# Groups of four in a two-layer conditional MLP: diagonal blocks summed in PSUM, off-diagonal banks begun by VectorE, and sums of shared matrices kept in DRAM

## The chip, the cores and the metric

The kernel runs on one core of one Trainium2 chip. The metric is the device time in microseconds, the median over runs. A profile of one execution comes beside it: it records every instruction of the engines TensorE (PE, with its weight loads as PEld), VectorE (DVE), ScalarE (ACT), GpSimd (POOL) and of the queues that issue DMAs (SP above all).

## The reference, cut to what matters

There are 16 batches x[b] of 256 x 256 numbers and two layers, each added to x.

```python
# layer 0: one expert of 8 for each batch, width 512
up, gate = x @ Wu[e].T + bu[e], x @ Wg[e].T + bg[e]
x = x + (silu(up) * gate) @ Wd[e].T + bd[e]

# layer 1: the two best of 8 experts for each batch, width 1024, weights w,
# and one shared expert that every batch passes through
mlp = lambda x, g, u, d: (gelu(x @ g) * (x @ u)) @ d
x = x + sum(w[k] * mlp(x, *expert[k]) for k in range(2)) + mlp(x, *shared)
```

All of it is float32.

## The kernel before, in words

**Units.** The work is cut into units that share one weight matrix. A *pair* (class Pair) is two batches with the same expert; a *single* (class Single) is one batch. Pairs use a Strassen-like scheme: seven block products (STEPS) in place of eight, from sums of the weight blocks and sums of the data blocks. Layer 0 has 4 pairs and up to 3 more; layer 1 has 12 routed pairs and up to 4 more, and what is left over are singles. The data decide how many: the program has arms for each case (function arms), and here three more pairs of layer 0, three more of layer 1 and two singles of layer 1 run.

The shared expert of layer 1 needs no routing: 8 batches go through it as 4 *shared pairs* (`shared`, which take turns with the three additional pairs of layer 0), the other 8 as two *groups of four* (class Quad) at the end. So the order of the units is: the first two singles and four pairs of layer 0; shared pairs in turn with the additional layer 0 pairs; 15 routed pairs; a single; two groups of four; the last single.

**A quarter of a pair.** The weights of a unit come in quarters j (2 in layer 0, 4 in layer 1). For each, `load_q` loads 512 KB (tile q), `sums_q` has GpSimd form four sums of its blocks (tile s; the operations are lines 588 to 591 in `sums_a`), `up` issues the seven products, and ScalarE (`copy`, L619) and VectorE (`combine`, L627) take the results out of PSUM into c. `act` applies gelu (L684) and the product with the other half (L690), `act_sums` forms three sums of the result with VectorE (`sums_b`, lines 581 to 583). `down` (L728) issues the seven products of the second matrix d, whose sums ds come from `sums_d`, again lines 588 to 591.

**A group of four** multiplies four blocks by four in 26 products instead of 32 (list BLOCK), twice (g = 0, 1). P_i and Q_i give block (i, i) as P_i + Q_i. For each pair i < j the product W goes into a bank that already holds a P (a *seed*, or P itself), ScalarE copies that bank to a second one (L1020), and the products N_ij and N_ji go on top of one bank each; VectorE then closes each with a subtraction (L930). Before the change, P_i and Q_i lie in banks of their own, VectorE adds them for the diagonal block, GpSimd makes "diagonal minus P" for blocks below it (L1012), and ScalarE writes the seeds (L973). `act` of the group takes a finished 2 x 2 of blocks through gelu (L942) and product (L943), and `act_sums` runs `sums_b` on GpSimd, for the second half of the last group on VectorE. The sums of the data blocks are `sums_r` (L868, L870) and `sums` (L883 to L885). The second half of the first group holds its triples back (`self.second`) until the downs of the first half are over.

**What sets the order.** The program is scheduled by hand. Class Line keeps a clock: `main` issues the next product of TensorE and moves the clock on, `later(after, f)` puts f behind that many units (one unit is one matmul call of 256 columns), and `ahead` issues, at the start of each quarter, the loads and sums for later quarters: q five quarters ahead, sums and x three ahead. Each engine works its instructions off in that order. Nearly all loads are issued on SP; the stores that add to the result are issued on GpSimd (L550). PSUM has eight banks, handed out by `bank` in the order in which they were released.

Of the kernel before, what the change touches and what calls it, by code (L numbers as in the profile page):

```python
# [62 lines left out]
SEED, MEAN = "S", "W"  # L63
BLOCK = (
    "P0", "P1", "Q0", "W01", "P2", "Q1", "P3", "N01", "N10", "Q2", "W23", "Q3",
    "W02", "W12", "N23", "N32", "N02", "N20", "W03", "N12", "N21", "W13",
    "N03", "N30", "N13", "N31",
)
SEEDS = {"Q2": ("02",), "W23": ("12",), "N32": ("03",), "N20": ("13",)}
# [6 lines left out]
def kernel(  # L76
# [22 lines left out]
    factors = [dram.tile([P, QW], F32, name=f"factors{j}") for j in range(CHUNKS)]  # L99

# [95 lines left out]
    psum = {"idle": list(range(NBANKS)), "filled": [False] * NBANKS}  # L196
    open_banks = {}

    def bank(of, seeded=False, half=False):
        ok = [i for i in psum["idle"] if psum["filled"][i] or not seeded]  # L200
        i = ok[0]
        psum["idle"].remove(i)
        assert of not in open_banks
        open_banks[of] = i
        psum["filled"][i] = not half
        return banks[i]
# [356 lines left out]
    class Pair(Unit):  # L563
# [3 lines left out]
        first, step = 18, None  # L567
# [10 lines left out]
        @staticmethod  # L578
        def sums_b(t, more, t2, engine=nc.vector):
            tt = engine.tensor_tensor  # L580
            tt(more[:, 0:2, :], t[:, 0:3:2, :], t[:, 2:4, :], ALU.subtract)  # L581
            tt(t2, t[:, C22, :], more[:, 0, :], ALU.add)  # L582
            tt(more[:, 2, :], t[:, C21, :], t2, ALU.subtract)  # L583
# [9 lines left out]
        def sums_q(self, j):  # L593
            s = take("s", QB, of=(self, j))
            s = s[:, :QW].rearrange("p (m k h) -> p m k h", m=2, k=4)
            self.s[j] = s
            q = self.q[j]
            self.sums_a(lambda n: q[:, :, A_AT[n], :], lambda n: s[:, :, S_AT[n], :])

        def sums_d(self):  # L600
            s = take("ds", 4, KPS[1], P, of=self)
            self.ds = s[:, :, : self.kp]
            d, s = self.d, self.ds
            self.sums_a(lambda n: d[:, A_AT[n]], lambda n: s[:, S_AT[n]])

# [112 lines left out]
        def down(self, k):  # L718
# [55 lines left out]
            elif k == 2:  # L774
                early(C12)
            elif k == 4:
                early(C22)
                early(C21)
                done_with((self, "X"))
                late(C22, "Q", -1)  # L780
# [3 lines left out]
            elif k == 6:  # L784
                late(C12, "Q", -1)
                done_with((self, "Q"))
# [15 lines left out]
        def run(self, line, among):  # L802
# [22 lines left out]
            for k in range(7):  # L825
                line.later(self.first + step * k, lambda k=k: self.down(k))

    class Quad(Unit):
# [32 lines left out]
        def sums_r(self):  # L861
# [3 lines left out]
            for i, k in enumerate(RATIOS):  # L865
# [6 lines left out]
        def sums(self, i, j):  # L872
# [10 lines left out]
            v.scalar_tensor_tensor(both, b["P", i], -1.0, b["P", j], ALU.mult, ALU.subtract)  # L883
            v.scalar_tensor_tensor(one, b["Q", j], -d, both, ALU.mult, ALU.add)
            v.scalar_tensor_tensor(two, b["Q", i], d, both, ALU.mult, ALU.add)  # L885
            b["W", i, j], b["N", i, j], b["N", j, i] = both, one, two

        def first_sums(self):
            if hasattr(self, "xb"):
                self.sums_r()  # L890
                self.sums(0, 1)
# [9 lines left out]
        def sums_d(self):  # L901
            self.ds = take("ds", 4, self.kd, P, of="quads")
            d, s = self.d, self.ds
            Pair.sums_a(lambda n: d[:, A_AT[n]], lambda n: s[:, S_AT[n]])

        def start(self):
            self.bank, self.copies, self.c, self.left, self.second = {}, {}, {}, {}, []
            for h in self.halves:
                h.start()
# [15 lines left out]
        def drop(self, g, *names):  # L925
            for n in names:
                give("cp4", (self, g, n))

        def close(self, g, i, j, dst, a, src, op):
            nc.vector.tensor_tensor(dst, a, src, op)  # L930
            at = g, i // 2, j // 2
            self.left[at] -= 1
            if self.left[at] == 0:
                line.later(3 * UP, lambda: when_free("at", lambda: self.act(*at)))

        def act(self, g, half, pair):
# [11 lines left out]
            if pair == 0 or h.sums_in == "sx":  # L948
                line.later(3 * UP, sums)
# [3 lines left out]
        def act_sums(self, h, j, t):  # L953
            more = take(h.sums_in, 3, S, of=(h, j))
            h.acts[j] = t, more
            engine = nc.vector if h.sums_in == "sx" else nc.gpsimd
            Pair.sums_b(t, more, t[:, 2, :], engine)
# [13 lines left out]
        def seed(self, g, i, j):  # L971
            x = bank((self, g, "X", i, j), seeded=True)
            nc.scalar.activation(x, self.copies[g, f"P{j}"], AF.Copy)  # L973
            self.bank["X", i, j] = x

        def product(self, n):
# [6 lines left out]
            def mm(dst, fresh):  # L983
# [6 lines left out]
            sub, add = ALU.subtract, ALU.add  # L990
            cp = self.copies
            if kind == "P":
                (i,) = ij
                of = (self, g, "X", i, i + 1) if i % 2 == 0 else (self, g, name)
                t = bank(of)
                mm(t, True)
                self.copy(g, name, t)
                if i % 2 == 0:
                    self.bank["X", i, i + 1] = t
                else:  # L1000
                    done_with(of)
            elif kind == "Q":
                (i,) = ij
                t = bank((self, g, name))
                mm(t, True)
                if i != 2:
                    self.copy(g, name, t)
                dst = self.block(g, i, i)
                self.close(g, i, i, dst, cp[g, f"P{i}"], t, add)
                done_with((self, g, name))  # L1010
                for k in ((1,), (), (3, 0, 1), (0, 1))[i]:
                    nc.gpsimd.tensor_tensor(self.block(g, k, i), dst, cp[g, f"P{k}"], sub)  # L1012
                if i == 3:
                    self.drop(g, "P0", "P1")
            elif kind == "W":
                i, j = ij
                x = self.bank["X", i, j]
                mm(x, False)
                y = bank((self, g, "Y", i, j), seeded=True)
                nc.scalar.activation(y, x, AF.Copy)  # L1020
                self.bank["Y", i, j] = y
            else:
                i, j = ij
                lo, hi = min(ij), max(ij)
                inside = hi - lo == 1 and lo % 2 == 0
                which = "X" if inside == (i < j) else "Y"
                t = self.bank.pop((which, lo, hi))
                mm(t, False)
                dst = self.block(g, i, j)
                self.close(g, i, j, dst, cp[g, f"Q{j}"] if which == "X" else dst, t, sub)  # L1030
                done_with((self, g, which, lo, hi))
                for q, last in (("Q1", "N31"), ("Q0", "N30"), ("Q3", "N23")):
                    if name == last:
                        self.drop(g, q)
            for pair in SEEDS.get(name, ()):
                self.seed(g, *map(int, pair))
                if pair == "12":
                    self.drop(g, "P2")
                elif pair == "13":
                    self.drop(g, "P3")  # L1040

        def run(self, line, among):

            self.start()
            while not hasattr(self, "b"):
                line.clock += 1
                line.flush(line.clock)
                self.first_sums()
# [4 lines left out]
            if self is quads[-1]:  # L1053
                give("xb", "quads")
                self.halves[-1].last = True
                if self.alone:
                    line.later(22 + 6 * 5, self.halves[-1].load_z)
            for i, h in enumerate(self.halves):
                for k in range(7):
                    line.later(22 + 6 * (7 * i + k), lambda h=h, k=k: self.down(h, k))  # L1060
# [5 lines left out]
    class Single(Unit):  # L1066
# [75 lines left out]
        def piece(self, line, j, among=False):  # L1142
# [5 lines left out]
            if self.layer:  # L1148
                line.later(SINGLE_UP, lambda: self.down(j))
# [154 lines left out]
    class Line:  # L1304
# [15 lines left out]

        def flush(self, until):
# [8 lines left out]
        def ahead(self, i):  # L1330
# [31 lines left out]
            if u.width == 4:  # L1362
                if j == 0:
                    self.later(0, lambda: u.sums(2, 3))
# [227 lines left out]
```

## Time and profile before

| | us |
|---|---|
| median of 3 runs (1054.15 to 1056.24) | 1054.78 |
| the profiled execution | 1053.92 |
| its span, first to last instruction | 1052.3 |
| end of the last matmul record in the span | 1046.3 |
| TensorE busy | 1030.9 |
| VectorE busy | 788.4 |
| GpSimd busy | 627.5 |
| ScalarE busy | 381.8 |
| bytes moved by DMA, MB (not us) | 143.37 |

The span is shorter than the time by 1.6 us, which lies around the first and the last instruction. Every matmul call leaves two records, so the 4714 records are about 2360 calls; in an undisturbed stretch one record follows the other by 0.216 us, and a call takes 0.43. Durations of matmuls in the tables are longer than that since consecutive ones overlap. A group of lines gives line, engine, operation, what is written and read, and the mean time of one; an arrow in brackets names what ended the idle time ahead of an instruction.

### The profile page before, as it was taken

The numbers are of one execution on the slowest core, as the hardware profiler recorded it, in microseconds if no ns is written. First come the engines' busy times: TensorE is split into PE (matmuls) and PEld (weight loads), VectorE is DVE, ScalarE is ACT, GpSimd is POOL, SyncE is SP. The second block draws the span as 40 slices with busy tenths as digits, with TensorE's granted clock in tenths as the row PEclk, the third lists the DMA queues.
The fourth block names the chain that finished last, engine by engine and source line by source line (L and its number), as shares of the span: only waits on it lengthen the run. The fifth ranks groups of instructions, "written<-read, shape, count | busy, mean of one in ns | idle before, by whom it ended". The sixth has DMA issues, their size and how long they took to land.

```text
span 1052.3 us, 14470 instructions
## 1 busy us (share of the span) xinstructions
PE 1030.9 (98%) x4714; PEld 896.9 (85%) x4714; DVE 788.4 (75%) x1206; ACT 381.8 (36%) x609; POOL 627.5 (60%) x672
## 2 busy tenths in 40 slices
PE   9999999899999999999999999999999999989997
PEld 7888788787878888888888888888888888878786
DVE  8898999879787878878777777778777655685351
ACT  2444353434333333333333333333333314544310
POOL 3955657465474889789567557737763203944821
PEclk9999999999999999999999999999999999999999
DMA  7645515344363665566235534524442364733414
GB/s 267 216 141 184 179 61 160 101 126 154 102 178 140 156 185 146 176 184 175 84 98 140 140 100 101 141 95 115 134 133 88 90 182 133 200 117 100 130 21 75
DMA packets 67508, 143.37 MB, mean 136 GB/s; under 512 B 7890, under 2 KB 38482, under 8 KB 64594
## 3 DMA queue, kind: packets, MB, share of 16 engines
q1 hardware_dynamic: 54866, 129.89, 37.0%
q0 software_dynamic: 12256, 12.06, 9.5%
q8 instruction: 43, 0.70, 0.3%
q14 instruction: 55, 0.45, 0.2%
q10 hardware_dynamic: 288, 0.26, 0.1%
HBM read 114.41 MB, written 27.79 MB: 135 GB/s over the span
## 4 chain that ended last, share of the span: by engine, by line
PE 81%; DVE 8%; POOL 4%; issue 3%; DMA 3%; ACT 1%; SPq 0%; POOLq 0%; DVEq 0%; ACTq 0%
PE bank L642 45%; PE bank L728 27%; PE bank L985 5%; PE bank L1075 3%; DVE c L627 2%; PE bank L1108 1%; DMA d<-wd_dram 1%; DVE bt L690 1%; DVE bt L943 1%; DVE bt L581 1%; DVE bt L582 1%; POOL d L1012 1%; PE bank L224 1%; POOL bt L582 0%; DMA out_dram<-ys 0%
## 5 line engine op out<-in xcount | busy, mean ns | idle before, releaser
L619 ACT ACTIVATE cp<-bank 128x512 f32<-128x512 f32 x270 | 160.9, 596 | 424.3 <-PE bank L642 423.7
L642 PE MATMUL bank<-xt,s 128*128 128x256 f32 x1216 | 288.7, 380 | 7.5 <-DVE c L627 7.5
L642 PEld LDWEIGHTS bank<-xt,s 128*128 128x128 f32 x1216 | 230.1, 190 | 42.3 <-issue 8.0
L627 DVE TENSOR_TENSOR c<-cp,bank 128x512 f32<-128x512 f32 x360 | 233.4, 678 | 31.0 <-ACT cp L619 17.9
L642 PE MATMUL bank<-xt,q 128*128 128x256 f32 x912 | 219.7, 379 | 0.0
L728 PE MATMUL bank<-bt,ds 128*128 128x256 f32 x816 | 196.2, 379 | 2.8 <-POOL bt L582 2.3
L642 PEld LDWEIGHTS bank<-xt,q 128*128 128x128 f32 x912 | 173.3, 190 | 23.6
L690 DVE TENSOR_TENSOR bt<-c 128x1024 f32<-128x1024 f32 x90 | 129.7, 1442 | 78.4 <-ACT c L684 75.9
L728 PEld LDWEIGHTS bank<-bt,ds 128*128 128x128 f32 x816 | 154.7, 190 | 25.1 <-POOL bt L582 2.7
L591 POOL TENSOR_TENSOR s<-s,q 128x256 f32<-128x256 f32 x90 | 77.6, 862 | 121.8 <-PE bank L642 121.8
L588 POOL TENSOR_TENSOR s<-q 128x256 f32<-128x256 f32 x90 | 90.8, 1008 | 86.3 <-PE bank L642 55.8
L728 PE MATMUL bank<-bt,d 128*128 128x256 f32 x572 | 137.0, 379 | 0.0
L728 PEld LDWEIGHTS bank<-bt,d 128*128 128x128 f32 x572 | 108.8, 190 | 15.0 <-DVE c L930 0.2
L550 POOL DMA_DIRECT2D out_dram<-ys x46 | 50.3, 1217 | 91.2 <-DVE ys L757 60.2
L589 POOL TENSOR_TENSOR s<-s,q 128x256 f32<-128x256 f32 x90 | 86.9, 965 | 7.1
L590 POOL TENSOR_TENSOR s<-q 128x256 f32<-128x256 f32 x90 | 86.5, 961 | 0.4 <-PE bank L642 0.4
L684 ACT ACTIVATE c<-c 128x1024 f32<-128x1024 f32 x76 | 79.9, 1052 | 12.5 <-DVE c L627 12.4
L581 DVE TENSOR_TENSOR bt<-bt 128x512 f32<-128x512 f32 x97 | 79.2, 817 | 0.3 <-DMA bt<-x_dram 0.3
L583 DVE TENSOR_TENSOR bt<-bt 128x256 f32<-128x256 f32 x90 | 63.6, 707 | 3.1
L582 DVE TENSOR_TENSOR bt<-bt 128x256 f32<-128x256 f32 x90 | 59.3, 659 | 3.1
L985 PE MATMUL bank<-xt,q 128*128 128x256 f32 x224 | 51.5, 380 | 2.7 <-DVE c L930 2.7
L985 PEld LDWEIGHTS bank<-xt,q 128*128 128x128 f32 x224 | 42.4, 190 | 8.9 <-DVE c L930 3.1
(212 smaller groups left out, 1109.0 us busy)
## 6 DMA issues: line engine op xcount, KB each, us to landing
q<-wq_dram SPq DMA_DIRECT2D x98, 512.0 KB, 3.6
d<-wd_dram SPq DMA_DIRECT2D x19, 1024.0 KB, 6.1
q<-factors SPq DMA_DIRECT2D x26, 512.0 KB, 3.3
xt<-x1d SPq DMA_DIRECT2D x46, 256.0 KB, 5.2
out_dram<-ys POOLq DMA_DIRECT2D x46, 256.0 KB, 6.0
d<-wd_dram SPq DMA_DIRECT2D x7, 513.0 KB, 5.2
bt<-x_dram SPq DMA_DIRECT2D x14, 256.0 KB, 4.6
x1d<-ys SPq DMA_DIRECT2D x14, 256.0 KB, 2.8
```

The source lines that it names most:

```text
L581: tt(more[:, 0:2, :], t[:, 0:3:2, :], t[:, 2:4, :], ALU.subtract)
L588: tt(s("S1"), a("A21"), a("A22"), ALU.add)
L589: tt(s("S2"), s("S1"), a("A11"), ALU.subtract)
L590: tt(s("nS3"), a("A21"), a("A11"), ALU.subtract)
L591: tt(s("nS4"), s("S2"), a("A12"), ALU.subtract)
L619: nc.scalar.activation(t, self.banks["X", j], AF.Copy)
L627: nc.vector.tensor_tensor(self.c[j][:, block].rearrange("p m s -> p (m s)"), self.copies[n, j], self.banks[tag, j], op,)
L642: nc.tensor.matmul(self.banks[tag, j][:, bass.ts(m, S)], lhsT=self.q[j][:, m, A_AT[a], :] if a in A_AT else self.s[j][:, m, S_AT[a], :], r ...
L684: nc.scalar.activation(u, u, AF.Gelu_apprx_tanh)
L690: nc.vector.tensor_tensor(t[:, 0:4, :], u, v, ALU.mult)
L728: nc.tensor.matmul(d, lhsT=src[:, j, :], rhs=self.act_block(j, b), start=OPENS[k] and j == 0, stop=j == self.kp - 1, skip_group_check=True,)
L985: nc.tensor.matmul(dst[:, bass.ts(m, S)], lhsT=w[:, m, :], rhs=rhs, start=fresh and m == 0, stop=True, skip_group_check=True,)
```

## The change

In the shared pairs, only the first computes the sums s and ds; GpSimd stores them to DRAM, and the other three shared pairs load them on SP's queue. The groups of four load ds too.

In the groups of four Q_i accumulates on P_i's bank, so a bank holds the whole diagonal block; ScalarE copies it once for the later subtractions and once more into c (`whole`). Every one of the six W banks is now begun by VectorE as P_i + P_j (`seed`); GpSimd's "diagonal minus P" goes. `act_sums` is VectorE's throughout. The order BLOCK, the seeds' places, the times of the data sums (SUMS_AT, now in single steps), of the activation (ACT_AT, ACT_SUMS_AT) and the order and times of the first group's downs (DOWNS, DOWNS_AT) are new. The downs get banks of their own around the groups (`psum["halves"]`), the last pair's downs come closer together (first 14, step 3), the first group waits until the pairs' downs are issued, and the last single's downs come four units later.

```diff
+BLOCK = ('P0', 'P1', 'P2', 'Q0', 'P3', 'W01', 'Q1', 'Q2', 'W02', 'N01', 'N10', 'Q3', 'W23', 'N02', 'N20', 'W12', 'N32', 'N23', 'W13', 'W03', 'N21', 'N13', 'N12', 'N03', 'N31', 'N30')
+SEEDS = {'P1': ('01',), 'P2': ('02',), 'W02': ('23',), 'Q3': ('12',), 'W12': ('03',), 'N10': ('13',)}
+SUMS_AT = ((4, (0, 2)), (4, (1, 2)), (10, (2, 3)), (22, (1, 3)), (30, (0, 3)))
+DOWNS = (0, 2, 4, 1, 5, 3, 6)
+DOWNS_AT = (8, 11, 12, 15, 19, 25, 27, 27, 33, 39, 46, 48, 49, 50)
+ACT_AT, ACT_SUMS_AT = 10, 6
...
+    qsums = [dram.tile([P, QW], F32, name=f"qsums{j}") for j in range(KPS[1])]
+    dsums = dram.tile([P, 4 * KPS[1] * P], F32, name="dsums")
...
     def bank(of, seeded=False, half=False):
         ok = [i for i in psum["idle"] if psum["filled"][i] or not seeded]
+        if psum["halves"]:
+            ok = [i for i in ok if (i in psum["halves"]) == half]
...
         def sums_q(self, j):
...
+            if self.at is None and self is not shared[0]:
+                nc.sync.dma_start(flat, qsums[j])
+                return
             q = self.q[j]
             self.sums_a(lambda n: q[:, :, A_AT[n], :], lambda n: s[:, :, S_AT[n], :])
+            if self is shared[0]:
+                nc.gpsimd.dma_start(qsums[j], flat)
...
+            if self.apart_banks:
+                line.later(self.first - 2, lambda: psum.update(
+                    halves=sorted(psum["idle"], key=lambda i: psum["filled"][i])[:3]
+                ))
...
-                line.later(3 * UP, lambda: when_free("at", lambda: self.act(*at)))
+                line.later(ACT_AT, lambda: when_free("at", lambda: self.act(*at)))
...
-            engine = nc.vector if h.sums_in == "sx" else nc.gpsimd
-            Pair.sums_b(t, more, t[:, 2, :], engine)
+            Pair.sums_b(t, more, t[:, 2, :])
...
             x = bank((self, g, "X", i, j), seeded=True)
-            nc.scalar.activation(x, self.copies[g, f"P{j}"], AF.Copy)
+            p = [self.copies[g, f"P{k}"] for k in (i, j)]
+            nc.vector.tensor_tensor(x, *p, ALU.add)
...
+        def whole(self, g, i):
+            nc.scalar.activation(self.block(g, i, i), self.copies[g, f"Q{i}"], AF.Copy)
...
             elif kind == "Q":
-                (i,) = ij
-                t = bank((self, g, name))
-                mm(t, True)
-                if i != 2:
-                    self.copy(g, name, t)
-                dst = self.block(g, i, i)
-                self.close(g, i, i, dst, cp[g, f"P{i}"], t, add)
-                done_with((self, g, name))
-                for k in ((1,), (), (3, 0, 1), (0, 1))[i]:
-                    nc.gpsimd.tensor_tensor(self.block(g, k, i), dst, cp[g, f"P{k}"], sub)
+                t = self.bank.pop(ij)
+                mm(t)
+                self.copy(g, name, t)
+                done_with((self, g, *ij))
+                line.later(0, lambda: self.whole(g, *ij))
...
-            while not hasattr(self, "b"):
+            while not hasattr(self, "b") or self is first_quad and line.busy(Pair):
...
-            for i, h in enumerate(self.halves):
-                for k in range(7):
-                    line.later(22 + 6 * (7 * i + k), lambda h=h, k=k: self.down(h, k))
+            for n in range(14):
+                i, k = divmod(n, 7)
+                h = self.halves[i]
+                at = 22 + 6 * n if self is quads[-1] else 2 * DOWNS_AT[n] + 2
+                k = k if self is quads[-1] else DOWNS[k]
+                line.later(at, lambda h=h, k=k: self.down(h, k))
...
-                line.later(SINGLE_UP, lambda: self.down(j))
+                line.later(SINGLE_UP + 4 * bool(self.x_from), lambda: self.down(j))
...
+            last_pair = [*tails[1], *more_pairs[:k]][-1]
+            last_pair.first, last_pair.step, last_pair.apart_banks = 14, 3, True
```

`sums_d` is changed as `sums_q` is, with dsums; in the groups of four it is one load of dsums.

## Prediction, made before the changed kernel was built or run

> **What bounds the kernel now.** I read the page first: busy shares, then the chain.
>
> ```profile
> PE 1030.9 (98%) x4714; PEld 896.9 (85%) x4714; DVE 788.4 (75%) x1206; ACT 381.8 (36%) x609; POOL 627.5 (60%) x672
> ...
> PE 81%; DVE 8%; POOL 4%; issue 3%; DMA 3%; ACT 1%; SPq 0%; POOLq 0%; DVEq 0%; ACTq 0%
> ```
>
> TensorE (PE) is the bound, and the change keeps its work: both orders of BLOCK hold 26 products (8 P and Q, 6 W, 12 N), each two matmuls. So the only thing to win is time in which PE waits or runs slowly. The view of waits, kept to PE, says where that is (total, times, longest):
>
> ```profile
> PE bank L642 <- DVE c L627: 7.5, 6, 2.7
> PE bank L985 <- DVE c L930: 2.7, 1, 2.7
> PE bank L728 <- POOL bt L582: 2.3, 1, 2.3
> ```
>
> Stretches of 20 us place them (stretch, its length, then busy time and count of PE, PEld, DVE, ACT, POOL, the granted clock, DMA share, GB/s). Undisturbed stretches hold 93 to 95 matmul records, these fewer:
>
> ```profile
> 120.00:140.00 20.00, 17.85 (x81) 14.61 (x80) 18.60 (x26) 9.74 (x15) 11.32 (x13) 1.00 0.51 171
> ...
> 180.00:200.00 20.00, 17.32 (x72) 14.40 (x71) 18.54 (x27) 9.94 (x15) 11.67 (x14) 0.91 0.47 158
> ...
> 240.00:260.00 20.00, 18.25 (x82) 15.16 (x82) 18.64 (x23) 10.25 (x15) 13.73 (x15) 1.00 0.37 124
> ...
> 920.00:940.00 20.00, 17.01 (x77) 14.18 (x76) 19.44 (x34) 9.79 (x17) 7.26 (x7) 0.99 0.42 138
> ```
>
> The first three lie where shared pairs alternate with layer 0's pairs, the fourth in the groups of four. In all four VectorE (DVE) is busy over 90%. From 420 to 840, in the routed pairs, PE never waits.
>
> Why is VectorE late there? Its timeline ahead of the wait that ends at 128.51 (start, length), and GpSimd's (POOL) beside it:
>
> ```profile
> 122.63 0.69 DVE L581 TENSOR_TENSOR bt<-bt 128x512 f32<-128x512 f32 x1
> 123.35 0.83 DVE L582 TENSOR_TENSOR dz<-bt 128x256 f32<-128x256 f32 x1
> 124.22 0.84 DVE L583 TENSOR_TENSOR bt<-bt,dz 128x256 f32<-128x256 f32 x1
> 124.98 1.75 DVE L1428 TENSOR_TENSOR z<-z,ys 128x1024 f32<-128x1024 f32 x1
> 126.65 1.21 DVE L690 TENSOR_TENSOR bt<-c 128x1024 f32<-128x1024 f32 x1
> ```
>
> ```profile
> 123.17 0.73 POOL L588 TENSOR_TENSOR s<-q 128x256 f32<-128x256 f32 x1 [0.94 <-PE bank L642]
> 123.98 0.79 POOL L589 TENSOR_TENSOR s<-s,q 128x256 f32<-128x256 f32 x1
> 124.74 0.91 POOL L590 TENSOR_TENSOR s<-q 128x256 f32<-128x256 f32 x1
> ```
>
> L582 and L583 take 0.43 when GpSimd is silent (at 120.63 and 121.09) and twice that here; 1024 elements take 1.21 alone (L690) and 1.75 beside L590. VectorE and GpSimd slow each other when both read SBUF.
>
> **Shared pairs: sums loaded instead of computed.** Counting L588 in order, the sums at 123 are those of the second shared pair, at 174 to 184 of the third, at 240 to 243 of the fourth: all three become loads. Removed from GpSimd: 12 quarters x 4 operations of about 0.95 (L588 to L591) = 45 us, and 3 x 5.4 = 16 us of L588 to L591 on ds. What PE gets back, wait by wait:
> - at 126: 0.40 + 0.41 + 0.54 = 1.35 of a wait of 1.82. VectorE has no gap since 112, where another L583 took 0.83, so I take 1.6;
> - at 184: the L583, L582, L583 from 179.81 each lose 0.41 and the L690 at 175.29 (1.57) 0.36: 1.6 of 2.68. An L581 of 1.52 at 167.12 lay beside the same pair's ds sums; I take 2.1;
> - at 243: 0.47 + 0.53 + 0.54 are more than the wait of 1.50: 1.5;
> - waits of 0.20, 0.33 and 0.24 at 175, 135 and 252, and 0.82 at 301 (behind an L583 of 1.38 beside ds sums that go): 1.3 of 1.59, the rest lying beside GpSimd work that stays.
>
> After the wait at 184 PE itself is slower:
>
> ```profile
> 187.28 1.10 PE L642 MATMUL bank<-xt,s 128*128 128x256 f32 x4 [2.68 <-DVE c L627]
> 188.22 1.58 PE L642 MATMUL bank<-dz,s 128*128 128x256 f32 x4
> 189.60 3.06 PE L642 MATMUL bank<-bt,s 128*128 128x256 f32 x8
> ```
>
> Elsewhere four records take 1.03 and eight 1.89, so this costs 0.55 + 1.17 = 1.7. Of the waits, the two of 2.68 (here and at 935) were followed by this, those of 2.32 and 1.82 were not. With 2.1 gone the wait is 0.6, so I count the 1.7 too. Together 1.6 + 2.1 + 1.5 + 1.3 + 1.7 = **8.2 us**; bounds 4.5 (1.35 + 1.6 + 1.5, clock and the rest unchanged) and 9.3 (all of it).
>
> The Trainium skill (TensorE: Matmul & The Clock Gate, Part 1) has the clock halve only after an idle window of about 3.4 us. By it a wait of 2.68 would not do this and the two slow stretches (3.4 us in all) would stay, leaving 10.8 of the 14.2 worked out here; the rows show slow matmuls behind exactly these two waits, and I go by them.
>
> Added: 12 loads of 512 KB, 4 of 1 MB, and one store of each sum. Today's q loads land 3.6 us after issue, d loads 6.1; these are issued three quarters before use, some 27 us (q loads follow each other about 9 us apart). DMA's share in the three stretches above is 0.37 to 0.51. All go through SP's queue, where the next q load stands behind them; it is five quarters early, and the slot they wait for was freed before the q slot that SP waits for already (539.8 us of SP's waits are that). The five stores cost GpSimd about 1.2 us each (L550). I cost all this at nothing; without that cover one late load is 3.6 us.
>
> **Groups of four.** Their waits: 0.31 at 920, 2.68 at 935, 2.32 at 978, and behind 935 eight records in 3.57 instead of 1.89, 1.7 us; with slow restarts (0.3) 7.3 us. The wait at 935 ends behind a burst of L883 to L885, two of them 1.38 and 1.49 instead of 0.42, beside GpSimd's L1012 and L581; the new SUMS_AT spreads these sums, and both GpSimd operations go. The wait at 978 is for GpSimd's L582, postponed sums of the second half.
>
> What VectorE takes over. The stretch of the products today:
>
> ```profile
> 870.00:1001.00 131.00, 125.69 (x573) 109.18 (x572) 79.73 (x121) 55.37 (x93) 80.39 (x68) 0.99 0.45 132
> ```
>
> Off VectorE: 16 diagonal closes of 0.685 = 11.0, and the slowing of L884, L885 and L943 (2.3 + 1.1 + 2.4 by their means against 0.42 and 1.23) = 5.8. On it: 24 seeds and 12 triples of L581 to L583. A sum of two SBUF tensors into a bank is not in the trace: below it 0.42 (256 elements), above it 0.82 (L581 on bt); I take 0.685 of L930, same shape and one bank: 16.4 (10 to 20). A triple is 1.52 from start to start where GpSimd is silent (1001.89 to 1003.41): 18.2. Net +17.8, so 97.5 busy. Without its waits PE needs 131 - 7.3 = 123.7, so VectorE fills 79%.
>
> ScalarE loses 16 seeds and gains 4 copies of Q and 16 block copies: 4 x 0.6 = 2.4 us on top of 55.4. GpSimd loses 24 L1012 and 12 triples, nearly all it does here.
>
> [...]
>
> What is late next: the four postponed triples, now one VectorE burst of 4 x 1.52 = 6.1 in the second group. The next seed behind it, after an activation product of 1.2, has until W02: six products of 0.86 and three downs of 1.73 = 10.4 us. The burst, product and seed need about 8.5 after the late sum in front. So close, but covered. The downs get two banks of their own, and k=4 stands one product (0.86) behind k=2, whose ScalarE copy takes 0.38 plus what is queued: a few tenths, twice. I charge 1.3 for such new waits: **6.0 us** gained, bounds 7.3 gained and, below, 17.8 lost.
>
> The last pair's downs move from steps of 6 to 3; PE does the same work there without waits today (845 to 900 is full), so nothing. The last single's downs come four units later, but its last still stands between the same two downs, so the chain that ends the kernel (its store, the z load, 0.2 of wait) stays.
>
> **Sum.** The profiled execution took 1053.92 (span 1052.3 and 1.6 around it). 1053.92 - 8.2 - 6.0 = 1039.7; the median of the runs shown is 0.86 higher: **1040.6**.
>
> **Rivals.**
> - *VectorE becomes the bound of the groups.* Today it idles 51.3 of the 131 us, in order behind PE, ScalarE's copies and gelu. If those waits stay while its work grows by 17.8, the stage takes 148.8 and the kernel 1039.7 + 6.0 + 17.8 = 1063.5, or 1064.4. For it: the waits on gelu (8.4) and copies (7.0) are real ones; most new work stands in the same queue as the closes that free banks. Against: over half of its idle time is waiting for PE, which more work simply fills. Slower than before from 42 us of remaining waits (97.5 + 42 = 131 + 8.5).
> - *The groups break even* (33.5 us of waits remain): 1039.7 + 6.0 + 0.9 = 1046.6.
> - *The shared stage gains nothing*, since GpSimd's remaining sums move into the same places or the loads hold SP up: 1039.7 + 8.2 + 0.9 = 1048.8. For it: at 301 and 308 PE waits behind sums that stay. Against: at 184 and 243 no other sums are ready to run.
> - *It does neither*: waits move only: 1054.8.
>
> **Chances.** Forecast 0.57, break-even groups 0.16, no gain in the shared stage 0.13, neither 0.05, VectorE-bound 0.09. A measurement of this kernel can tell about 0.2% (2.1 us) from no change. Faster 0.86, same 0.05, slower 0.09. The range goes from all listed waits gone (9.3 + 7.3: 1038.2) less 1.2 for what the views don't list, 1037.0, to just past the third case, 1049.5; 0.14 is left out.
>
> **What would show it.** Right: PE waits on L627 between 110 and 260 fall below 2 us, L582 and L583 there near 0.43; 93 or more records in each stretch of the groups; VectorE near 80% busy there. Wrong: new waits of PE for a seed or for s loaded from qsums, SP's q loads landing late, VectorE over 95% in the groups.

## The result, and the profile after

The changed kernel takes **1035.46 us** (median of 4 runs, 1034.93 to 1035.97) beside 1054.47 for the kernel before on the same chip (4 runs, 1052.51 to 1056.24). The ratio is 0.982, 95% interval 0.9802 to 0.9839: faster by 1.8%. The prediction was 1040.6 with a range of 1037.0 to 1049.5. Its direction and its places held, its size did not: 19.0 us came where 14.2 were forecast, and the time lies 1.5 us below the range.

The profiled execution took 1034.93 with a span of 1033.3. Its busy shares, and the shares of the chain that ended last:

```profile
PE 1025.3 (99%) x4714; PEld 894.5 (87%) x4714; DVE 786.9 (76%) x1250; ACT 384.0 (37%) x613; POOL 494.3 (48%) x553
...
PE 93%; DVE 3%; POOL 2%; issue 1%; ACT 0%; DMA 0%; SPq 0%; POOLq 0%; DVEq 0%; ACTq 0%
```

TensorE issues the same 4714 records and is 5.6 us less busy. By the starts of the records some 3.4 us of that are the slow matmuls behind the waits at 184 and 935; most of the rest lies at the stops that are gone. (The profile ends a record 0.38 us after its start, where normally the next one starts after 0.216; so 0.17 us of a stop count as busy, and the record behind the stop takes 0.1 longer.) The remaining gain is waiting, and the whole list of TensorE's waits above 0.2 us is now this (total, times, longest):

```profile
PE bank L231 <- DVE cp L228: 1.6, 1, 1.6
PE bank L660 <- DVE c L645: 1.2, 3, 0.5
PE bank L746 <- DVE dz L763: 0.3, 1, 0.3
PE bank L660 <- ACT cp L637: 0.2, 1, 0.2
```

The first, at the very start, was there before. The 7.5 us behind `combine` became 1.2; the waits for L930 and for GpSimd's triples have no successor at all, and no wait for a seed is listed. By stretches, in the places that the prediction showed (columns as there), and then the whole stretch of the groups' products:

```profile
120.00:140.00 20.00, 20.00 (x92) 16.83 (x91) 18.48 (x29) 11.37 (x17) 4.18 (x5) 1.00 0.73 257
...
180.00:200.00 20.00, 19.50 (x89) 16.47 (x88) 17.87 (x27) 9.89 (x17) 6.62 (x7) 1.00 0.61 205
...
240.00:260.00 20.00, 20.00 (x93) 17.46 (x93) 16.47 (x23) 11.45 (x18) 7.89 (x9) 1.00 0.51 185
...
920.00:940.00 20.00, 20.00 (x94) 17.62 (x93) 16.63 (x33) 10.66 (x20) 0.00 (x0) 1.00 0.29 97
```

```profile
860.80:984.30 123.50, 123.50 (x574) 108.63 (x573) 93.42 (x166) 58.15 (x97) 6.05 (x6) 1.00 0.52 154
```

TensorE fills them but for 0.5 us in the second. GpSimd's time fell from between 11.3 and 13.7 us to between 4.2 and 7.9 in the first three, and to nothing in the fourth. The DMA share rose (0.51 to 0.73 in the first) without a wait for it. In the groups VectorE is busy 93.4 of 123.5 us, 76%; the prediction said 97.5 and 79%. VectorE's timeline at the place shown before (start, length):

```profile
122.34 0.69 DVE L588 TENSOR_TENSOR bt<-bt 128x512 f32<-128x512 f32 x1
123.06 0.42 DVE L589 TENSOR_TENSOR dz<-bt 128x256 f32<-128x256 f32 x1
123.52 0.42 DVE L590 TENSOR_TENSOR bt<-bt,dz 128x256 f32<-128x256 f32 x1
123.86 1.22 DVE L1459 TENSOR_TENSOR z<-z,ys 128x1024 f32<-128x1024 f32 x1
125.00 1.22 DVE L708 TENSOR_TENSOR bt<-c 128x1024 f32<-128x1024 f32 x1
```

Same operations, same order: 0.83, 0.84 and 1.75 have become 0.42, 0.42 and 1.22.

**Where the 19.0 us lie.** Both kernels issue the same number of matmul records, so the n-th record's start can be compared. The lead of the changed kernel:

| up to | lead, us | gained there |
|---|---|---|
| record 500 (115 us) | -0.33 | |
| record 1400 (313 us; shared stage) | 9.49 | 9.8 |
| record 4100 (896 us; routed pairs, start of the groups) | 9.49 | 0 |
| record 4500 (982 us; groups) | 17.33 | 7.8 |
| the last record | 17.67 | 0.3 |
| end of execution | 19.0 | 1.3 |

The last 1.3 lie behind the last matmul: 5.96 us before, 4.63 after. In the profiles of this study that stretch is 4.5 to 6.3 us long, longest in e10, which ends as the changed kernel does. So no run shows that the change has a part in these 1.3.

### The profile page after: what moved, and what is told of

Its sections match the earlier page's. It is cut to its first block, busy times and chain, and to the rows that moved or that the text cites. A ratio compares the mean times of both kernels' runs of the same rounds, so it can differ in the third digit from the quotient of the medians.

```text
span 1033.3 us, 14372 instructions
## 1 busy us (share of the span) xinstructions
PE 1025.3 (99%) x4714; PEld 894.5 (87%) x4714; DVE 786.9 (76%) x1250; ACT 384.0 (37%) x613; POOL 494.3 (48%) x553
## 4 chain that ended last, share of the span: by engine, by line
PE 93%; DVE 3%; POOL 2%; issue 1%; ACT 0%; DMA 0%; SPq 0%; POOLq 0%; DVEq 0%; ACTq 0%
PE bank L660 48%; PE bank L746 30%; PE bank L1030 9%; PE bank L1103 4%; PE bank L1136 2%; DVE c L645 1%; DVE bt L708 1%; PE bank L231 1%; POOL s L595 0%; DMA bt<-x_dram 0%; POOL s L597 0%; POOL s L598 0%; DVE bt L588 0%; POOL s L596 0%; ACT c L702 0%
## 5 line engine op out<-in xcount | busy, mean ns | idle before, releaser
L645 DVE TENSOR_TENSOR c<-cp,bank 128x512 f32<-128x512 f32 x360 | 233.9, 679 | 35.1 <-ACT cp L637 17.7
L660 PEld LDWEIGHTS bank<-xt,q 128*128 128x128 f32 x912 | 173.3, 190 | 23.6
L595 POOL TENSOR_TENSOR s<-q 128x256 f32<-128x256 f32 x78 | 77.8, 998 | 82.7 <-PE bank L660 49.7
L598 POOL TENSOR_TENSOR s<-s,q 128x256 f32<-128x256 f32 x78 | 66.2, 849 | 98.0 <-PE bank L660 91.3
L588 DVE TENSOR_TENSOR bt<-bt 128x512 f32<-128x512 f32 x105 | 81.9, 780 | 0.5 <-DMA bt<-x_dram 0.5
L596 POOL TENSOR_TENSOR s<-s,q 128x256 f32<-128x256 f32 x78 | 77.5, 994 | 6.1
L597 POOL TENSOR_TENSOR s<-q 128x256 f32<-128x256 f32 x78 | 74.1, 950 | 0.2 <-PE bank L660 0.2
L595 POOL TENSOR_TENSOR ds<-d 128x512 f32<-128x512 f32 (+1 forms) x21 | 24.7, 1178 | 79.1 <-DMA d<-wd_dram 51.0
```

What stands on the lines that cost most here:

```text
L595: tt(s("S1"), a("A21"), a("A22"), ALU.add)
L596: tt(s("S2"), s("S1"), a("A11"), ALU.subtract)
L597: tt(s("nS3"), a("A21"), a("A11"), ALU.subtract)
L598: tt(s("nS4"), s("S2"), a("A12"), ALU.subtract)
L645: nc.vector.tensor_tensor(self.c[j][:, block].rearrange("p m s -> p (m s)"), self.copies[n, j], self.banks[tag, j], op,)
L660: nc.tensor.matmul(self.banks[tag, j][:, bass.ts(m, S)], lhsT=self.q[j][:, m, A_AT[a], :] if a in A_AT else self.s[j][:, m, S_AT[a], :], r ...
```

## The experiments

All times are medians, and ratios stand against the kernel before on the same chip. "After" is the changed kernel, 1035.5. The kernel before took 1055.1 to 1056.2 beside the experiments and 1054.5 beside the changed kernel, so a difference of two medians can be off by a microsecond. The tables therefore also give what TensorE loses in the groups by record starts, in us: how much later record 4600 starts, less how much later record 3000 does (record 4000 against e1).

### Sums loaded, alone

`e1_stored_sums` is the kernel before with qsums and dsums as in the change and nothing else. `e2_groups_only` is its complement: the changed kernel, sums computed everywhere.

```diff
+            if self.at is None and self is not shared[0]:
+                nc.sync.dma_start(flat, qsums[j])
+                return
```

> The kernel before with the stored sums alone. My theory (GpSimd's sums slow VectorE, so their removal frees TensorE in the shared stage, whatever the groups do): the waits of TensorE on L627 between 110 and 260 fall from 6.0 us to under 1, no slow stretch of matmuls near 184, and the time falls by the 9.5 us that the two profiles show up to the groups: 1045.0, between 1044 and 1046.5. Rival (the loads hold SP up, and only the freed groups hide it): 1049 or more, with q loads landing late.

> The changed kernel with the sums of all shared pairs, and of the groups' ds, computed by GpSimd again. My theory (the two parts are independent): the groups keep 7.8 us and the end 1.7 at most, the shared stage gives its 9.5 back: 1045.0, between 1043.5 and 1047. Rival (part of the shared stage's gain comes from the new order, not from the stored sums): 1036 to 1041.

Measured: e1 1043.04, ratio 0.9881 (0.986 to 0.9903); e2 1046.78, ratio 0.9908 (0.9885 to 0.9931). TensorE's waits in the groups of e1, and in the shared stage of e2:

```profile
PE bank L999 <- DVE c L944: 2.7, 1, 2.7
PE bank L743 <- POOL bt L586: 2.3, 1, 2.3
```

```profile
PE bank L649 <- DVE c L634: 8.1, 6, 2.7
```

These are the waits of before, or nearly (8.1 us against 7.5), so neither half needs the other: by record starts 9.8 us of e1's gain lie in the shared stage and 7.5 of e2's in the groups. No wait of TensorE for a load is listed. e2 lies in the range expected, e1 1 us below it.

### What GpSimd did to VectorE: reading, writing, or filling its queue

Both kernels are the changed one, and their loads still deliver the sums. In e3, GpSimd first writes zeros over the places of the sums, twice; in e4 it computes the sums there, and the load then writes the same over them.

```diff
+                for n in ("S1", "S2", "nS3", "nS4"):        # e3
+                    for _ in range(2):
+                        nc.gpsimd.memset(s[:, :, S_AT[n], :], 0.0)
+                self.sums_a(lambda n: q[:, :, A_AT[n], :], lambda n: s[:, :, S_AT[n], :])   # e4
```

> The changed kernel, with GpSimd filling the same places of s and ds with zeros, twice, ahead of each load, which then overwrites them: GpSimd is busy at the same points, behind the same slots, and only writes; the loads come as late as GpSimd is. My theory (it is GpSimd's reading of SBUF beside VectorE's two SBUF inputs that costs): L589 and L590 stay near 0.43, time within 1.5 us of 1035.5. Rivals (any GpSimd work there slows VectorE; or it is the lateness of the sums that TensorE feels): 1041 to 1046.

> The changed kernel, with GpSimd computing the sums of the shared pairs as before, and the loads overwriting them with the same numbers afterwards. Differs from the run with zeros only in what GpSimd reads. My theory: L589 and L590 in the shared stage go to 0.6 to 0.7 on average, the waits on VectorE come back, 1043.5 to 1047. Rival (GpSimd's reads don't matter): the same time as the run with zeros.

Measured: e3 1035.61, ratio 0.9808 (0.9788 to 0.9828); e4 1046.89, ratio 0.9911 (0.9883 to 0.9938). Both lie where expected. The group of GpSimd's writes in e3 and of one of VectorE's operations (100 to 260 us), then the same operation and TensorE's wait in e4:

```profile
L607 POOL MEMSET s<- 128x256 f32 x96 | 29.6, 325 | 34.3 <-PE bank L666 31.5
```

```profile
L590 DVE TENSOR_TENSOR bt<-bt 128x256 f32<-128x256 f32 x18 | 9.4, 523 | 0.6
```

```profile
L590 DVE TENSOR_TENSOR bt<-bt 128x256 f32<-128x256 f32 x17 | 12.2, 718 | 0.6
```

```profile
PE bank L663 <- DVE c L648: 8.3, 6, 2.7
```

The same line's mean is 451 ns in the changed kernel. The 523 of e3 do not come from the writes: GpSimd still computes the sums of layer 0's pairs there, and every one of these operations that took longer lay beside such a sum. From e3's timelines, an operation beside writes and one beside sums:

```profile
123.55 1.92 POOL L607 MEMSET s<- 128x256 f32 x6 [1.05 <-PE bank L666]
123.58 0.42 DVE L590 TENSOR_TENSOR bt<-bt,dz 128x256 f32<-128x256 f32 x1
```

```profile
136.61 1.18 POOL L597 TENSOR_TENSOR ds<-d 128x256 f32<-128x256 f32 x1
137.23 0.84 DVE L589 TENSOR_TENSOR xt<-xt 128x256 f32<-128x256 f32 x1
```

From 100 to 260 us, the 18 VectorE sums of this size that lay beside writes and beside no sum of GpSimd's took 0.42 to 0.43 us, and TensorE loses nothing in e3. In e4 the median of the 36 beside GpSimd's sums is 0.83, and the whole 11 us come back. That is more than the 9.8 gained, because the first wait (at 129) grew to 2.4 us and slow matmuls followed it. That GpSimd's queue is full, so that sums come late, is hardly the cause: GpSimd is busy for 78.2 of these 160 us in e3 and for 94.7 in e4 (43.4 in the changed kernel), and 8.3 us of e4's waits end at VectorE's `combine`, 0.7 at a sum and none at a load. So the shared stage's gain is that GpSimd no longer reads SBUF beside VectorE. The Trainium skill (SBUF — State Buffer, "SBUF: two separate sides") says that a VectorE operation with two SBUF inputs and a GpSimd operation that reads SBUF shut each other out for a whole instruction. The 0.42 beside writes against 0.83 beside sums agree, and so do the closes of e11 below, which read one input from PSUM and keep their 0.68.

### The groups, one part at a time undone

```diff
-            Pair.sums_b(t, more, t[:, 2, :])                         # e5: triples on GpSimd
+            Pair.sums_b(t, more, t[:, 2, :], engine)                 #     (last half: VectorE)
-                at = 22 + 6 * n if self is quads[-1] else 2 * DOWNS_AT[n] + 2   # e6: plain downs
-                k = k if self is quads[-1] else DOWNS[k]
+                at = 22 + 6 * n
-                    for k, (at, of) in enumerate(SUMS_AT):           # e7: data sums in threes,
+                    for of in ((2, 3),):                             #     at their old places
```

> The changed kernel with the groups' triples of sums (all but the last group's second half) on GpSimd again, as before the change; order, seeds and diagonal as changed. My theory (GpSimd's reading slows VectorE's seeds, products and data sums, and GpSimd itself is late with the four postponed triples): waits of TensorE return in the groups, one of about 2 us for L589 on GpSimd and some behind VectorE; 1038 to 1042.5. Rival (the new order and the spread sums did it): within 1.2 of 1035.5.

> The changed kernel with the first group's downs in the old order 0 to 6 and at the old even steps of six. My theory (the groups gain by what GpSimd no longer does; order and places of the downs save little): 1035 to 1037, at most 1.3 us of waits, which is what I charged for the new order. Rival (the new places are what hides the burst of four triples): a wait of 2 us or more in the second group, 1037.5 or more.

> The changed kernel with the sums of the data blocks at the places they had before (all of the first pair's at once, (2, 3) at the start of a group, the others three units apart in the second quarter). The wait of 2.68 at 935 held 2.44 of slowing beside GpSimd, by the rows of before. My theory: with GpSimd silent the bursts alone cost at most 1 us: 1035 to 1036.5. Rival (the burst is the cause, whoever runs beside it): 2.5 us and more: 1038 to 1040.

| | us | ratio (interval) | against after | by record starts |
|---|---|---|---|---|
| e5 | 1037.51 | 0.9825 (0.9808 to 0.9841) | +2.0 | 1.7 |
| e6 | 1035.97 | 0.981 (0.9794 to 0.9827) | +0.5 | 0.0 |
| e7 | 1036.75 | 0.9816 (0.98 to 0.9832) | +1.3 | 2.3 |

Each part undone costs little, and two expectations were missed by a little (e5 cost less than thought, e7 more, and by record starts nearly what its rival said). They do not add up to 7.8.

### The groups, one part at a time done

So the other direction: e1 (1043.04, old order) and, on top of it, the triples on VectorE (e8), the subtractions L1012 as well (e9); the spread data sums instead (e13), and all three (e12).

```diff
-            Pair.sums_b(t, more, t[:, 2, :], engine)                             # e8, e9, e12
+            Pair.sums_b(t, more, t[:, 2, :])
-                    nc.gpsimd.tensor_tensor(self.block(g, k, i), dst, cp[g, f"P{k}"], sub)  # e9, e12
+                    nc.vector.tensor_tensor(self.block(g, k, i), dst, cp[g, f"P{k}"], sub)
-                    self.later(0, lambda: u.sums(2, 3))                          # e12, e13
+                    for k, (at, of) in enumerate(SUMS_AT):
+                        for step in range(3):
+                            self.later(at + 2 * step, lambda of=of, s=step: u.sums(*of, s))
```

> The kernel before with the stored sums (1043.0) and, of the groups' changes, only the triples on VectorE; GpSimd keeps its diagonal subtractions L1012 of before, the order stays. My theory: the wait for GpSimd of 2.3 us in the second group goes, the one of 2.7 behind the burst shrinks by the part of the slowing that lay beside L581: 1038.5 to 1041.5. Rival (VectorE cannot take the triples without the new order): 1043 or more.

> The kernel before with stored sums (stored sums alone: 1043.0 us), and in its groups of four the triples and the 24 subtractions 'diagonal minus P' (L1012) both on VectorE, the old order kept. GpSimd then computes nothing beside the groups' products. If GpSimd's reading beside VectorE is what the groups' waits are made of, the triples go back to 0.69 + 0.42 + 0.42, no other VectorE operation is slowed, and the waits of 2.6 us and more go: 1037 to 1041. My theory after the run with the triples alone on VectorE (1044.9): the old order gives VectorE its work in bursts, and 24 x 0.685 = 16 us more of them outweigh the contention that goes (about 10 us), so VectorE is some 103 us busy of 124, the waits stay, and the kernel takes 1044 to 1050. Slower than the kernel before (1054.8) would be the rival in which VectorE becomes the bound of the groups.

> The kernel before with stored sums (alone: 1043.0 us) and one part of the change in the groups of four: the data sums in single steps at the changed kernel's times. Old order, GpSimd's work as before. What the prediction said of the wait of 2.7 us (burst of data sums ahead of a close): it goes, and with it the slow matmuls behind it, 4.5 us in all, while the wait of 2.3 us for GpSimd's postponed triples stays: 1038 to 1040. The rival, that the order sets the waits: VectorE's closes come as late for other reasons and the wait moves: 1042 to 1045.

> The same two parts (stored sums, data sums spread), and in the groups the triples and the subtractions L1012 on VectorE (without the spread: 1045.6 us), old order. VectorE's work is as in the run without the spread, about 108 of 140 us. If the burst is what makes TensorE wait there (2.4 us and slow matmuls behind it, 4.8 us in all), 1039 to 1041.5. If VectorE's load in the old order makes the waits, they move: 1043.5 to 1046.5.

| | us | ratio (interval) | against e1 | by record starts |
|---|---|---|---|---|
| e8 | 1044.91 | 0.9896 (0.9879 to 0.9912) | +1.9 | 1.7 |
| e9 | 1045.56 | 0.992 (0.9901 to 0.9938) | +2.5 | 1.9 |
| e13 | 1046.76 | 0.9913 (0.9888 to 0.9939) | +3.7 | 3.8 |
| e12 | 1046.03 | 0.9915 (0.9893 to 0.9937) | +3.0 | 2.9 |

Nothing helps; e8 and e13 went against what I had expected. (The intervals overlap e1's; that the groups became slower is said by the record starts.) In the kernel before, two of the data sums ahead of the late close had been slowed, beside GpSimd's L1012 and L581:

```profile
931.82 1.38 DVE L884 SCALAR_TENSOR_TENSOR s<-xt,s 128x256 f32<-128x256 f32 x1
933.12 1.49 DVE L885 SCALAR_TENSOR_TENSOR s<-xt,s 128x256 f32<-128x256 f32 x1
```

In e9 GpSimd computes nothing beside the products, and yet TensorE waits 2.4 us at 929. VectorE's timeline before the close that ends this wait:

```profile
925.30 0.68 DVE L944 TENSOR_TENSOR c<-spare,bank 128x512 f32<-128x512 f32 x1
925.90 0.42 DVE L898 SCALAR_TENSOR_TENSOR s<-xt 128x256 f32<-128x256 f32 x1
926.35 0.42 DVE L899 SCALAR_TENSOR_TENSOR s<-xt,s 128x256 f32<-128x256 f32 x1
926.69 0.42 DVE L900 SCALAR_TENSOR_TENSOR s<-xt,s 128x256 f32<-128x256 f32 x1
927.03 0.42 DVE L898 SCALAR_TENSOR_TENSOR s<-xt 128x256 f32<-128x256 f32 x1
927.48 0.42 DVE L899 SCALAR_TENSOR_TENSOR s<-xt,s 128x256 f32<-128x256 f32 x1
927.82 0.42 DVE L900 SCALAR_TENSOR_TENSOR s<-xt,s 128x256 f32<-128x256 f32 x1
928.15 0.68 DVE L944 TENSOR_TENSOR c<-cp,bank 128x512 f32<-128x512 f32 x1
```

Every operation runs at its undisturbed length, back to back since 911. The close comes late because six data sums (and before them activation products and a triple) stand ahead of it in one queue. Spread, in e13, the sums are late themselves: TensorE waits for two of them (L904), and a close (L955) is late as well. The spread's times are those made for the new order; a spread made for the old order was not tried.

```profile
PE bank L1010 <- DVE xt L904: 2.9, 1, 2.9
PE bank L744 <- POOL bt L587: 2.3, 1, 2.3
...
PE bank L744 <- DVE c L955: 1.5, 1, 1.5
PE bank L1010 <- DVE s L904: 1.1, 1, 1.1
```

### The order of products, and GpSimd's reading within it

e10 is the changed kernel with the old list BLOCK; e14 has the activation at its old time as well. Seeds 01 and 23 stand at the first product at which both of their P are there. The other four stand where the kernel before has them, which is later than that and not what the expectation says. The times of the data sums and of the downs stay those made for the new order. e11 is the changed kernel with GpSimd subtractions beside it, whose result nobody reads: nearly as many elements as the L1012 of before.

```diff
-BLOCK = ('P0', 'P1', 'P2', 'Q0', 'P3', 'W01', 'Q1', ...                # e10, e14
+BLOCK = ("P0", "P1", "Q0", "W01", "P2", "Q1", "P3", "N01", ...
+SEEDS = {"P1": ("01",), "P3": ("23",), "Q2": ("02",), "W23": ("12",), "N32": ("03",), "N20": ("13",)}
-ACT_AT, ACT_SUMS_AT = 10, 6                                            # e14
+ACT_AT, ACT_SUMS_AT = 3 * UP, 6
+                nc.gpsimd.tensor_tensor(scratch, q[:, part], p[:, part], ALU.subtract)   # e11
```

> The changed kernel (1035.5 us) with the order of products of before, each seed at the earliest product at which both of its P are there. All other parts of the change stay. Same amount of work on every engine. If the order carries part of the gain: W01 then stands one product (0.86 us) behind the P1 whose copy its seed waits for, where copy 0.6 and seed 0.69 are 1.3 us and more, so TensorE waits up to 0.85 us there in each of the 4 runs through the list, and some more where several closes stand ahead of a seed: 1037 to 1042. The rival, that the diagonal in PSUM and the silent GpSimd make up the whole gain of the groups and the order nothing: 1035 to 1036.5.

> The changed kernel with the old order of products (with the new activation times: 1044.9 us), and the activation 6 units behind its last block, as before, in place of 10. It tells how much of that run's loss of 9.4 us is the order itself and how much are times that were fitted to another order. The waits of 0.47 us at the seeds of W01 must stay. My theory, that seeds queue behind closes in the old order whatever the activation does: 1043 to 1046. The rival, that the activation's products stand ahead of the seeds only because of its time: 1038 to 1042.

> The changed kernel (1035.5 us) and, beside it, subtractions on GpSimd of the same copies of P and Q into a tile that nobody reads, as many elements per run through the list (nearly: 448 of 512 columns, in pieces of 112) as the 'diagonal minus P' of before, issued as each diagonal block is copied. The output stays the same. It prices GpSimd's reading of SBUF beside VectorE within the new order. My theory: some 24 x 1.4 = 34 us of GpSimd reading slow the VectorE operations beside it by 8 to 12 us in all, VectorE is then about 104 of 124 us busy, and part of it reaches TensorE: 1036.5 to 1040. The rival, that with the new order the slack absorbs it: 1035 to 1036.

| | us | ratio (interval) | against after | by record starts |
|---|---|---|---|---|
| e10 | 1044.87 | 0.9908 (0.9892 to 0.9925) | +9.4 | 8.3 |
| e14 | 1042.96 | 0.9887 (0.9866 to 0.9909) | +7.5 | 7.8 |
| e11 | 1038.04 | 0.985 (0.9833 to 0.9866) | +2.6 | 1.7 |

e10 is 2.9 us slower than the range expected, e14 at the lower end of its own, e11 inside. TensorE's waits for seeds in e10 and in e14:

```profile
PE bank L1034 <- DVE bank L1016: 5.8, 8, 1.3
```

```profile
PE bank L1034 <- DVE bank L1016: 6.0, 5, 1.7
```

In e14, 3.8 of the 6.0 us are waits at W01 and 2.2 at W03; in e10, 1.4 are at W01 and 4.4 at W02, W03 and W13. One of those at W01 in e14, on three engines (start, length): the second run through the list.

```profile
896.01 1.05 ACT L985 ACTIVATE d<-d 128x1024 f32<-128x1024 f32 x1
896.96 0.59 ACT L964 ACTIVATE spare<-bank 128x512 f32<-128x512 f32 x1
```

```profile
897.10 1.23 DVE L986 TENSOR_TENSOR bt<-d 128x1024 f32<-128x1024 f32 x1 [1.75 <-ACT d L985]
898.24 0.69 DVE L1016 TENSOR_TENSOR bank<-spare 128x512 f32<-128x512 f32 x1
```

```profile
898.99 0.48 PE L1034 MATMUL bank<-xt,q 128*128 128x256 f32 x1 [1.69 <-DVE bank L1016]
```

The gelu of the run before stands ahead of P1's copy on ScalarE, and its product ahead of the seed on VectorE; W01, the fourth product, comes too early for that. In the new order W01 is the sixth: the same gelu and product are there, and a seed at 894.46 and one at 896.55 are done before TensorE gets to them.

```profile
894.46 0.70 DVE L1012 TENSOR_TENSOR bank<-spare 128x512 f32<-128x512 f32 x1 [0.92 <-ACT spare L960]
895.40 1.23 DVE L982 TENSOR_TENSOR bt<-d 128x1024 f32<-128x1024 f32 x1 [0.24 <-ACT d L981]
896.55 0.69 DVE L1012 TENSOR_TENSOR bank<-spare,xs 128x512 f32<-128x512 f32 x1
```

So with the old order and its seeds the other parts of the change gain nothing in the groups: e14 takes as long as e1 (1042.96 and 1043.04). That the order is needed is shown; that it would do alone is not, and neither is how much of the 7.5 us seeds, sums and downs placed for the old order would win back. GpSimd's subtractions of before, put back nearly in full, cost 2.6 us, 1.7 of them in the groups.

## Why the prediction came out as it did

**The sum.** 1040.6 was forecast, 5.1 us more than measured: 1.6 of these lie in the shared stage, 1.8 in the groups, 1.3 behind the last matmul and 0.3 in the kernel before, which took 1054.47 and not 1054.78. The range's low end, 1037.0, left room for a gain of 17.8 us, and TensorE's lead at its last record is 17.7; so what carried the time past it are the 1.3, which the sum put at nothing, and the 0.3. The two terms were too small all the same.

**The shared stage: right in cause and place, mis-sized.** The term was 8.2, the trace has 9.8. By record starts, in its own pieces: 126 and 135 gave 2.5 (1.6 + 0.33 counted), 175 and 184 with the slow clock 4.1 (0.20 + 2.1 + 1.7), 243 and 252 2.2 (1.5 + 0.24), 301 and 308 1.0 (about 0.5 of the small waits). The step that fell short is the reading of a listed wait as its whole price. A wait is counted from the end of the record before, which the profile puts 0.38 us after its start, where an undisturbed record follows after 0.216; so TensorE loses 0.17 us more than the list shows (the wait of 1.82 is a gap of 2.20 between starts, 1.98 lost; 0.33 is 0.49, 1.50 is 1.67). Six of the eight stops went, which makes 1.0 us. It was counted in the groups (0.3) and not here. The other 0.6 are waits that went further than counted: at 126 and in the small ones "I take 1.6" and "1.3 of 1.59" were cautious, while "I take 2.1" at 184 was right, for 0.50 of 2.68 stayed. The upper bound of 9.3 had the same hole.

**The groups: right in sign, its size off by 1.8, its reason incomplete.** The term was 7.3 less 1.3 for new waits, the trace has 7.8. "I charge 1.3 for such new waits" is the step that failed in size: none came, since the triples' burst was covered, as worked out, and the downs' times changed nothing (e6). The other 0.5 are what the three stops cost beside their waits, 2.5 us by record starts where 2.0 were counted. In reason, the step "The wait at 935 ends behind a burst of L883 to L885 ... the new SUMS_AT spreads these sums, and both GpSimd operations go" fell short. In the old order, with this spread and both GpSimd operations moved to VectorE, the kernel was slower than with stored sums alone (e12, +3.0; the spread by itself, e13, +3.7). e12 gives VectorE more work than the change does (95.9 of 124 us against 93.4 of 123.5); e14 does not (89.7 of 124) and says the same. What keeps VectorE in time is the order of the products together with the copies, seeds and closes placed to fit it, and the prediction took that order as given: it counted 26 products in both lists and went on.

**VectorE's load: right.** 76% against 79% forecast; a seed 0.694 against 0.685 charged; a triple 1.53. The rival "VectorE becomes the bound" was rightly held to be unlikely for this change, but waits of its kind exist: with 72 to 78% and another order, TensorE waits (e9, e10). Busy share did not tell these apart.

**Loads, tail, last single: right at nothing, as far as can be told.** The loads of the sums landed later than the rows of before said (5.8 and 7.4 us after issue, in place of 3.6 and 6.1), but no wait for them is listed. The end's 1.3 us are within what the profiles vary by.

**The slow clock.** Counting the slow matmuls behind the waits of 2.68 as part of their price was right for this kernel: they went. That they follow every such wait is not so: in e4 a wait of 2.67 was followed by matmuls at full speed, in e2 the wait at the same place by slow ones, as before. The granted clock from 187 to 195 us was 0.79 in the kernel before and in e2, 1.00 in e4.

```profile
189.32 1.10 PE L663 MATMUL bank<-xt,s 128*128 128x256 f32 x4 [2.67 <-DVE c L648]
```

```profile
189.43 2.05 PE L649 MATMUL bank<-xt,s 128*128 128x256 f32 x4 [2.67 <-DVE c L634]
```

The Trainium skill (TensorE: Matmul & The Clock Gate, Part 1) has an idle window of about 3.4 us that runs free of the kernel; slow matmuls behind 2.4 to 2.9 us of waiting contradict a full window of idleness, while their coming and going at the same length would fit a window that runs free. By its threshold no wait here would have mattered, and 3.4 us of this gain would not exist.

**Open.** Whether the new order alone, with Q in banks of its own and GpSimd's subtractions, would have gained was not tried: it needs another plan of banks. So how the groups' 7.8 us divide among the parts stays open. No run beat the changed kernel.

## What to carry to other kernels

Where VectorE paces TensorE, look first at what GpSimd reads beside it: results that are the same for several units can be computed once, stored and loaded, if DMA has room. When a product needs something that two in-order engines prepare, its place in the order can decide more than those engines' busy share, as it did here; a part of such a change tried alone, in the old order, can look like a loss. And a short stop of TensorE costs more than the listed wait (0.17 us here), and sometimes a slow stretch.

## What the runs showed of the hardware

- Beside GpSimd operations that read SBUF, VectorE's operations on two SBUF tensors, 128 x 256, went from 0.42 to 0.83 us (e4, median of 36). Those with one input in PSUM, 128 x 512, stayed at 0.68 (e11, where seeds of the same length rose from 695 to 773 ns):

```profile
L1013 DVE TENSOR_TENSOR bank<-cp,cp 128x512 f32<-128x512 f32 x9 | 7.0, 773 | 7.0 <-ACT cp L961 5.2 <-ACT spare L961 1.8
L1063 DVE TENSOR_TENSOR d<-spare,bank 128x512 f32<-128x512 f32 x10 | 6.7, 681 | 1.4 <-PE bank L1038 1.0 <-ACT bank L1057 0.3
```

- GpSimd writing alone (a memset of 128 x 256 in 325 ns) did not slow them: 0.42 to 0.43 us beside it (e3, 18 operations).
- A sum of two SBUF tensors into a PSUM bank, 128 x 512, takes 0.69, as long as one with an operand in PSUM.
- Slow matmuls, 0.43 us apart instead of 0.22 and at a granted clock of 0.57 to 0.67 over the 4 us behind the wait, followed ten of the eleven waits of 2.38 to 2.91 us in these profiles (two of 2.41 and 2.42, in e2 and e4, with no other wait near), not the one of 2.67 in e4 and none of the three of 2.32 and 2.33.
